# Attention over a sorted graph: VectorE weights edge one-hots two blocks at a time, ScalarE converts all node one-hots, stored as 8-bit floats beside the sum layers

## The chip, the cores and the metric

The kernel runs on one core of one Trainium2 chip. The metric is the device time of the whole program in microseconds, as the median of repeated executions. Beside the times there is one profiled execution, whose trace gives the start and the duration of every instruction. The engines are called PE (TensorE; PEld is its weight load), DVE (VectorE), ACT (ScalarE), POOL (GpSimd) and SP (the queue that issues most DMAs).

## The reference, cut to what matters

A graph of 6250 nodes with 128 features and 100,000 edges, sorted by destination, goes through four blocks, each a layer norm, a ReLU and a graph network, added to x: a mean over neighbours, a product over edges, three sum layers (mean over neighbours, two matrices each), and three attention layers. The last two are what matters here.

```python
def _sage_layer(x, src, dst, Wl, Wr, bias, n_nodes):          # the sum layers
    msg_sum = segment_sum(x[src], dst); cnt = segment_sum(1, dst)
    return (msg_sum / maximum(cnt, 1)) @ Wl + x @ Wr + bias

def _gat_conv(x, src, dst, ea, W, a_src, a_dst, We, a_edge, bias):   # attention, with self loops
    h = x @ W
    alpha = leaky_relu((h @ a_src)[s] + (h @ a_dst)[d] + ea_full @ We @ a_edge, 0.2)
    ex = exp(alpha - segment_max(alpha, d)[d])
    coef = ex / (segment_sum(ex, d)[d] + 1e-16)
    return segment_sum(h[s] * coef[:, None], d) + bias
```

The graph is the same in all three attention layers; only the coefficients change.

## The kernel before, in words

**The attention layers** (`attention_split`, `split_edges`). The edges are split. The destinations of the "late" edges are handled by gathering rows of a table from DRAM (POOL, L67), running a recurrence over them on DVE (`late`, `acc`, `ex`, `top`) and storing the history. The destinations of the "early" edges are handled with matrix products, and this is the part that the change touches. Their nodes lie in 5 groups (GP) of 128 windows; a window has 5 nodes (NW) and up to 128 edges (WCAP). For each window two one-hot matrices pick things out: `hot` has, for each edge, a one in the column that its source belongs to (125 columns of nodes), and the node one-hot has, for each edge, a one in column k*50+l of 250, where k is the destination within the window and l the rest of the source's number. `cnt = (hot * coef)^T @ node one-hot` is then a small weighted adjacency, which ACT merges into `m` (`merged`, L2607), and `product` (L2447) multiplies `m` with the features `hst` held in SBUF.

A loop of 160 steps per layer (480 in all) treats four windows a step. The windows alternate between two number formats: k = 0 is done in full F32, k = 1 in F32R as a high and a low part (`coef_h`, `coef_l`, so there is a third weighted one-hot, `hot_l`). `ready(step + 2)` makes the operands two steps ahead, into tiles with three buffers. Before the change, for each of the four windows it makes

- the node one-hot `hot_n`: for k = 0 DVE compares `l_slot` with the edge's place (`lt.id_t`, F32; L116), 250 elements; for k = 1 ACT converts an 8-bit one-hot `half_n` loaded from DRAM (L2435);
- the weighted edge one-hot `hot_c`: ACT multiplies the 8-bit `hot` with the coefficient of each edge (L2436), 125 elements;

and once a step, for both k = 1 windows together, DVE makes `hot_l` (L112, 250 elements). `nodes_ready` issues the loads: `hot` every second step, `half_n` every step (L2416, 62.5 KB).

Within a step the program order is: PE's products into `cnt` (two PSUM buffers), the start of a product unit, ACT's merge of the step before, `ready(step + 2)`, some matmuls of the product, the source terms or the softmax of the next group, then the gathers and the late recurrence. On PE, DVE and ACT this order is fixed: a function `chain` ties each instruction to the one before it on its engine. ACT thus takes the exponential of the late recurrence (L2502) in turn with the merges and the one-hots. The gathers on POOL are tied to PE's progress (`clocked`).

**Beside the sum layers** (`woven`). The one-hots don't depend on the features, so they are made earlier, by `early_edges`, while the three sum layers run. `woven` cuts each unit of a sum layer (four node tiles: some 120 matmuls into `o`, L1544) into 15 pieces and puts a piece of the side work, one `next(beside)`, after 9 of them; the end of the unit before (`node_terms`: `agg` on DVE, `nt` on PE, L1564, and then its norm or its split into parts) is spread over the first pieces. Again the order on PE, DVE and ACT is as written. The sum layers read their adjacency from DRAM through `piece` loads on SP (L1643), six buffers ahead, and ACT converts a part of them (`as_f`, L1653). Another recurrence on DVE (`s_acc`) uses gathered rows.

For each of the 80 blocks of 8 windows, `early_edges` makes on DVE `ee_hot` (8 compares of 128), `ee_col` (one TENSOR_TENSOR of 400 elements with both operands spread over two axes), `ee_node` (4 compares of 250, the k = 1 windows alone; L2028) and `ee_hot_t`, and stores each with a DMA on SP. All of these are tiles with two buffers. `slot_b` is the bf16 row 0, 1, 2, ... ; `place` holds each edge's column k*50+l and is transposed, per group, into `lt.id_t`.

Of the kernel before, what the change touches and what calls it, by code (L numbers as in the profile page):

```python
# [9 lines left out]
F32 = mybir.dt.float32  # L10
BF16 = mybir.dt.bfloat16
# [40 lines left out]
def kernel(ctx: ExitStack, tc: tile.TileContext, a: dict, out: bass.AP):  # L52
# [58 lines left out]
    def tt(o, x, y, op):  # L111
        nc.vector.tensor_tensor(o, x, y, op)  # L112
# [1715 lines left out]
    hot_t_dram = [dram.tile([128, 128 * 128], F8, name=f"hot_t{g}") for g in range(GP)]  # L1828
    col_dram = [dram.tile([128, 128 * T], F8, name=f"col{g}") for g in range(GP)]
    of_dram = [dram.tile([128, NW * WCAP], BF16, name=f"of{g}") for g in range(GP)]  # L1830
    node_dram = [dram.tile([128, 64 * T * NW], F8, name=f"node{g}") for g in range(GP)]
    ale_dram = [[dram.tile([128, WCAP], F32, name=f"ale{i}_{g}") for g in range(GP)] for i in range(3)]
    ade_dram = [dram.tile([PL * C2, 1], F32, name=f"ade{i}") for i in range(3)]
    part_dram = [dram.tile([128, WCAP], U8, name=f"part{g}") for g in range(GP)]
# [7 lines left out]
    class Late:  # L1842
# [3 lines left out]
        def __init__(self, pool):  # L1846
            self.y_t = pool.tile([128, T, P], F32, name="y_t")
            self.src = pool.tile([128, C2], I32, name="l_src")
            self.same = pool.tile([PL, C2], F32, name="l_same")
            self.pen = pool.tile([PL, C2], F32, name="l_pen")  # L1850
            self.first = pool.tile([PL, 1], I32, name="l_first")
            self.fix = pool.tile([PL, 1], I32, name="l_fix")
            self.flow_t = pool.tile([PL, PL], F32, name="l_flow_t")
            self.pen_t = pool.tile([PL, PL], F32, name="l_pen_t")
            self.end = pool.tile([128, T2], I32, name="l_end")
            self.q = pool.tile([R2, T2], F32, name="l_q")
            self.c = pool.tile([R2, T2], F32, name="l_c")
            self.slot = pool.tile([128, C2], F32, name="l_slot")
            self.id_t = pool.tile([128, GP, 128], F32, name="l_id_t")
            self.vecs = [pool.tile([128, 6], F32, name=f"l_vecs{i}") for i in range(3)]  # L1860
            self.w_ext = [pool.tile([128, W], F32, name=f"l_w_ext{i}") for i in range(3)]
            self.v = [pool.tile([128, 3], F32, name=f"l_v{i}") for i in range(3)]
            self.e_self = [pool.tile([128, 1], F32, name=f"l_e_self{i}") for i in range(3)]
            self.als = pool.tile([128, 3, 2, T], BF16, name="l_als")
# [162 lines left out]
    def one_hot(o, x, at):  # L2027
        nc.vector.tensor_scalar(o, x, at, None, op0=OP.is_equal, saturate=False)  # L2028

    def early_edges(lt):  # L2030

        with tc.tile_pool(name="ee", bufs=1) as pool, tc.tile_pool(name="ee_ps", bufs=1, space=PSUM) as ps:
# [59 lines left out]
            for g in range(GP):  # L2092
# [41 lines left out]
                yield  # L2134
                hi_t = f32("hi_t", 128)
                lo_t = pool.tile([128, 128], BF16, name="ee_lo_t")
                for x, x_t in ((hi, hi_t), (lo, lo_t), (place, lt.id_t[:, g, :])):
                    t_ps = ps.tile([128, 128], F32, name="ee_t")
                    transpose(t_ps, x)
                    nc.vector.tensor_copy(x_t, t_ps)  # L2140
                    yield
                rows = rows_of(g, 0)
                for w0 in range(0, 128, WB):
                    hot = pool.tile([128, WB, 128], F8, name="ee_hot", bufs=2)
                    for w in range(WB):
                        one_hot(hot[:, w, :], slot_b[:, :128], hi_t[:, w0 + w:w0 + w + 1])
                    nc.sync.dma_start(hot_dram[g][:, w0 * 128:(w0 + WB) * 128], hot.rearrange("p w h -> p (w h)"))
                    col = pool.tile([128, WB, T], F8, name="ee_col", bufs=2)
                    nc.vector.tensor_tensor(col, slot_b[:, None, :T].to_broadcast([128, WB, T]),
                                            lo_t[:, w0:w0 + WB, None].to_broadcast([128, WB, T]), OP.is_equal, saturate=False)  # L2150
                    nc.sync.dma_start(col_dram[g][:, w0 * T:(w0 + WB) * T], col.rearrange("p w l -> p (w l)"))
                    yield
                    node = pool.tile([128, WB // 2, T * NW], F8, name="ee_node", bufs=2)
                    for w in range(0, WB, 2):
                        n = w0 + w + 1
                        one_hot(node[:, w // 2, :], slot_b, lt.id_t[:, g, n:n + 1])
                    nc.sync.dma_start(node_dram[g][:, w0 // 2 * T * NW:(w0 + WB) // 2 * T * NW],
                                      node.rearrange("p w n -> p (w n)"))
                    hot_t = pool.tile([128, WB * WCAP], F8, name="ee_hot_t", bufs=2)
                    one_hot(hot_t, rows, here[:, 0:1])  # L2160
                    nc.sync.dma_start(hot_t_dram[g][:, w0 * 128:(w0 + WB) * 128], hot_t)
                    if w0 + WB < 128:
                        rows = rows_of(g, w0 + WB)
                    yield
# [105 lines left out]
    def split_edges(lt, i, first, wp, pool, ps, mv, sc):  # L2270
# [138 lines left out]
        def nodes_ready(step):  # L2409

            g, w0 = step // 32, step % 32 * 4
            if w0 % WB == 0:
                lt.hot = pool.tile([128, WB, 128], F8, name="hot")
                nc.sync.dma_start(lt.hot.rearrange("p w h -> p (w h)"), hot_dram[g][:, w0 * 128:(w0 + WB) * 128])
            half_n = pool.tile([128, 2, T * NW], F8, name="half_n")
            nc.sync.dma_start(half_n.rearrange("p w n -> p (w n)"),  # L2416
                              node_dram[g][:, w0 // 2 * T * NW:(w0 + 4) // 2 * T * NW])
            return half_n

        def ready(step, half_n=None):  # L2420

            g, w0 = step // 32, step % 32 * 4
            if half_n is None:
                half_n = nodes_ready(step)
            hot_n = [pool.tile([128, 2, T * NW], of, name=f"hot_n{k}", bufs=3) for k, of in enumerate((F32, F32R))]
            hot_c = [pool.tile([128, 2, P], of, name=f"hot_c{k}", bufs=3) for k, of in enumerate((F32, F32R))]
            hot_l = pool.tile([128, 2, P], F32R, name="hot_l", bufs=3)
            hot = lt.hot[:, w0 % WB:w0 % WB + 4, :P]
            coef, high, low = coef_t[g]
            for w in range(4):  # L2430
                k, h = w % 2, w // 2
                if k == 0:
                    ts(hot_n[k][:, h, :], lt.slot[:, :T * NW], lt.id_t[:, g, w0 + w:w0 + w + 1], OP.is_equal)
                else:
                    nc.scalar.activation(hot_n[k][:, h, :], half_n[:, h, :], AF.Copy)  # L2435
                nc.scalar.activation(hot_c[k][:, h, :], hot[:, w, :], AF.Copy,  # L2436
                                     scale=(high if k else coef)[:, w0 + w:w0 + w + 1])
            tt(hot_l, hot.rearrange("p (h k) c -> p k h c", k=2)[:, 1],
               low[:, w0:w0 + 4].rearrange("p (h k) -> p k h", k=2)[:, 1, :, None].to_broadcast([128, 2, P]), OP.mult)
            return hot_n, hot_c, hot_l  # L2440
# [704 lines left out]
```

## Time and profile before

| what | value |
|---|---|
| median of 13 runs | 4818.59 us (4804.71 to 4827.85) |
| the profiled execution | 4828.39 us |
| its span, first to last instruction | 4825.9 us, mean granted clock 0.895 |
| busy: PE, PEld, DVE | 4163.7, 2991.3, 4042.7 us |
| busy: ACT, POOL | 3308.4, 2849.0 us |
| sum layers (about 1880 to 2800 us), busy PE, DVE, ACT | 882, 679, 437 of 920 us |
| attention layers and the end (2800 to 4826 us), busy PE, DVE, ACT | 1801, 1700, 1514 of 2026 us |
| attention loops, first to last merge | 2862.8 to 3435.3, 3523.2 to 4095.3, 4184.4 to 4754.5 us |

How to read the lines of the profile: a row of the table of stretches gives the stretch, its length, each engine's busy time with the number of its instructions, the granted PE clock, the mean busy share of the 16 DMA engines and GB/s. A group gives line, engine and operation, out<-in by the program's names, the shapes and the count; then busy time and mean ns of one; then the idle time of the engine just before these instructions and what ended it. A wait line gives who waited for whom: us in total, times, longest. A line of the order of time gives start, us and the instruction. L112, L116, L118 and L121 are helpers (`tt`, `ts` and `stt`) that many places call, so there one goes by tile names. DVE and ACT instructions overlap at their ends, so that the mean of one is longer than the distance from start to start.

### The profile page before, as it was taken

The numbers are of one execution on the slowest core, as the hardware profiler recorded it, in microseconds if no ns is written. First come the engines' busy times: TensorE is split into PE (matmuls) and PEld (weight loads), VectorE is DVE, ScalarE is ACT, GpSimd is POOL, SyncE is SP. The second block draws the span as 40 slices with busy tenths as digits, with TensorE's granted clock in tenths as the row PEclk, the third lists the DMA queues.
The fourth block names the chain that finished last, engine by engine and source line by source line (L and its number), as shares of the span: only waits on it lengthen the run. The fifth ranks groups of instructions, "written<-read, shape, count | busy, mean of one in ns | idle before, by whom it ended". The sixth has DMA issues, their size and how long they took to land. (4 is left out here: it accounts for less than half of the span.)

```text
span 4825.9 us, 84662 instructions
## 1 busy us (share of the span) xinstructions
PE 4163.7 (86%) x25786; PEld 2991.3 (62%) x25786; DVE 4042.7 (84%) x12029; ACT 3308.4 (69%) x6467; POOL 2849.0 (59%) x2848
## 2 busy tenths in 40 slices
PE   1499998888888869999999979999789999799996
PEld 0255543434444435555555569889778898698895
DVE  7999869999999964678868869899698897798985
ACT  5466658888888856543345568778577787687784
POOL 1365007777777754656737537677377776477772
PEclk9999996666666659999999989999999999899998
DMA  4344236666666647899989955555455554465553
GB/s 99 102 153 163 92 118 215 206 203 201 197 202 206 184 131 226 265 282 279 297 243 297 282 167 160 157 154 155 138 150 156 156 159 132 148 164 154 156 148 106
DMA packets 577362, 868.53 MB, mean 180 GB/s; under 512 B 206555, under 2 KB 451739, under 8 KB 568450
## 3 DMA queue, kind: packets, MB, share of 16 engines
q1 hardware_dynamic: 483459, 674.15, 44.5%
q0 software_dynamic: 91104, 186.95, 15.8%
q8 instruction: 205, 3.36, 0.3%
q10 hardware_dynamic: 2332, 1.93, 0.2%
q14 instruction: 262, 2.15, 0.1%
HBM read 563.92 MB, written 298.68 MB: 179 GB/s over the span
## 5 line engine op out<-in xcount | busy, mean ns | idle before, releaser
L67 POOL DMA_INDIRECT rows<-gtable,l_src x1176 | 1187.2, 1010 | 547.5 <-issue 277.0
L67 POOL DMA_INDIRECT rows<-table,f_src x784 | 781.5, 997 | 282.2 <-issue 181.6
L2447 PE MATMUL o<-m,hst 125*128 125x160 f32 x6000 | 917.1, 304 | 0.0
L2624 PE MATMUL cnt<-hot_n,hot_c 128*125 128x250 f32 x2880 | 758.7, 361 | 121.0 <-ACT m L2607 117.2
L67 POOL DMA_INDIRECT s_rows<-table,s_src x660 | 661.3, 1002 | 340.7 <-issue 168.5
L2447 PEld LDWEIGHTS o<-m,hst 125*128 125x128 f32 x6000 | 856.0, 194 | 0.0
L1653 ACT ACTIVATE as_f<-piece 128x1000 fp32r<-128x1000 fp8e4 x390 | 381.5, 1029 | 278.0 <-DMA piece<-adj 180.8
L2624 PEld LDWEIGHTS cnt<-hot_n,hot_c 128*125 128x125 f32 x2880 | 452.1, 193 | 158.4 <-ACT m L2607 128.7
L2607 ACT ACTIVATE m<-cnt 125x1000 f32<-125x1000 f32 x480 | 474.3, 988 | 17.0 <-PE cnt L2624 15.8
L923 PE MATMUL z<-w,s 128*128 128x128 f32 x1568 | 348.1, 391 | 152.5 <-DVE s L121 148.1
L2623 PE MATMUL cnt<-hot_n,hot_l 128*125 128x250 f32 x960 | 454.6, 474 | 0.0
L121 DVE SCALAR_TENSOR_TENSOR acc<-acc,ex,rows 128x130 f32<-128x130 f32 x1173 | 414.4, 353 | 33.8
L923 PEld LDWEIGHTS z<-w,s 128*128 128x128 f32 x1568 | 295.3, 281 | 232.3 <-DVE s L121 231.9
L1544 PE MATMUL o<-as_f,of_two 128*128 128x500 f32 x1560 | 415.6, 412 | 12.7 <-ACT as_f L1653 12.5
L1407 ACT ACTIVATE adj<-cnt 128x1000 fp8e4<-128x1000 f32 x250 | 305.4, 1222 | 174.4 <-PE cnt L1406 168.5
L2435 ACT ACTIVATE hot_n<-half_n 128x250 fp32r<-128x250 fp8e4 x960 | 386.4, 402 | 28.2 <-DMA half_n<-node 27.5
L2436 ACT ACTIVATE hot_c<-hot,coef_t 128x125 f32<-128x125 fp8e4 x960 | 375.6, 391 | 0.1
L2436 ACT ACTIVATE hot_c<-hot,coef_h 128x125 fp32r<-128x125 fp8e4 x960 | 374.9, 391 | 0.0
L902 PE MATMUL z<-bf,w 128*128 128x512 f32 x392 | 354.2, 1002 | 9.0 <-ACT bf L868 9.0
L1544 PE MATMUL o<-adj,parts 128*128 128x500 fp8e4 x1500 | 357.0, 376 | 0.1
L1544 PEld LDWEIGHTS o<-as_f,of_two 128*128 128x128 f32 x1560 | 296.4, 192 | 84.0 <-ACT as_f L1653 16.4
L868 ACT ACTIVATE soft<-z 128x512 f32<-128x512 f32 x392 | 222.2, 586 | 164.5 <-PE z L923 164.0
(628 smaller groups left out, 8114.9 us busy)
## 6 DMA issues: line engine op xcount, KB each, us to landing
piece<-adj SPq DMA_DIRECT2D x360, 250.0 KB
late_hist<-acc SPq DMA_DIRECT2D x147, 455.0 KB
dist<-ew_dram SPq DMA_DIRECT2D x48, 1024.0 KB
sum_hist<-s_acc SPq DMA_DIRECT2D x132, 320.0 KB
adj<-adj SPq DMA_DIRECT2D x10, 3125.0 KB
hot<-hot SPq DMA_DIRECT2D x240, 128.0 KB
half_n<-node SPq DMA_DIRECT2D x480, 62.5 KB
ea<-in_edge_attr SPq DMA_DIRECT2D x54, 512.0 KB
```

Of the source, the lines that this page charges most:

```text
L67: return nc.gpsimd.indirect_dma_start(out=dst, out_offset=None, in_=table, in_offset=bass.IndirectOffsetOnAxis(ap=idx, axis=0))
L121: nc.vector.scalar_tensor_tensor(o, x, s, y, op0=op0, op1=op1)
L902: nc.tensor.matmul(z1, lhsT=w1, rhs=st["bf"][:, i % 2 * HB:(i % 2 + 1) * HB, :], start=False, stop=True)
L923: nc.tensor.matmul(z2[:, j, :], lhsT=s1[:, j, :], rhs=w2, start=False, stop=j == HB - 1)
L1544: yield nc.tensor.matmul(o[:, :n], lhsT=parts.columns(l, 1, s)[:, 0, :], rhs=adj(l), start=(l == 0 and s == 0), stop=(l == T - 1 and s == ...
L1653: nc.scalar.activation(made[-1], piece[:, at:at + n], AF.Copy)
L2435: nc.scalar.activation(hot_n[k][:, h, :], half_n[:, h, :], AF.Copy)
L2436: nc.scalar.activation(hot_c[k][:, h, :], hot[:, w, :], AF.Copy, scale=(high if k else coef)[:, w0 + w:w0 + w + 1])
L2447: nc.tensor.matmul(o, lhsT=hst[:, l, :D], rhs=m[:P, l, :], start=(l == 0), stop=(l == T - 1))
L2607: nc.scalar.activation(m[:P, :, :, u * 4:u * 4 + 4].rearrange("p l k q -> p k l q"), cnt[:P, :, :T * NW].rearrange("p w (k l) -> p k l w", ...
L2623: nc.tensor.matmul(o, lhsT=hot_l[:, h, :], rhs=hot_n[k][:, h, :], start=True, stop=False)
L2624: nc.tensor.matmul(o, lhsT=hot_c[k][:, h, :], rhs=hot_n[k][:, h, :], start=k == 0, stop=True)
```

## The change

It has two halves that belong together.

1. `early_edges` makes and stores the node one-hots of all 8 windows of a block instead of the four with k = 1. It no longer uses four compares with one number per partition, but two TENSOR_TENSOR compares of four windows each (128 x 1000 elements, 8-bit result), which compare `slot_b` with the edges' places held in bf16 (`id_b`). Each of the two results is stored with its own DMA. `ee_node` keeps two buffers of 1000 bytes a partition; the DRAM tensors `node` double, and `lt.id_t` goes.
2. `ready` no longer compares on DVE nor weights on ACT. ACT converts the node one-hots of both formats (two instructions of 500 elements, from `half_n` with four windows, 125 KB a load); DVE weights the edge one-hots (two TENSOR_TENSOR products of 2 x 125 elements, as `hot_l` has been made).

```diff
@@ early_edges
-                for x, x_t in ((hi, hi_t), (lo, lo_t), (place, lt.id_t[:, g, :])):
+                id_b = pool.tile([128, 128], BF16, name="ee_id_b")
+                for x, x_t in ((hi, hi_t), (lo, lo_t), (place, id_b)):
...
-                    node = pool.tile([128, WB // 2, T * NW], F8, name="ee_node", bufs=2)
-                    for w in range(0, WB, 2):
-                        n = w0 + w + 1
-                        one_hot(node[:, w // 2, :], slot_b, lt.id_t[:, g, n:n + 1])
-                    nc.sync.dma_start(node_dram[g][:, w0 // 2 * T * NW:(w0 + WB) // 2 * T * NW],
-                                      node.rearrange("p w n -> p (w n)"))
+                    for n0 in range(w0, w0 + WB, 4):
+                        node = pool.tile([128, 4, T * NW], F8, name="ee_node", bufs=2)
+                        nc.vector.tensor_tensor(node, slot_b[:, None, :].to_broadcast([128, 4, T * NW]),
+                                                id_b[:, n0:n0 + 4, None].to_broadcast([128, 4, T * NW]), OP.is_equal, saturate=False)
+                        nc.sync.dma_start(node_dram[g][:, n0 * T * NW:(n0 + 4) * T * NW], node.rearrange("p w n -> p (w n)"))
@@ nodes_ready
-            half_n = pool.tile([128, 2, T * NW], F8, name="half_n")
-            nc.sync.dma_start(half_n.rearrange("p w n -> p (w n)"),
-                              node_dram[g][:, w0 // 2 * T * NW:(w0 + 4) // 2 * T * NW])
+            half_n = pool.tile([128, 4, T * NW], F8, name="half_n")
+            nc.sync.dma_start(half_n.rearrange("p w n -> p (w n)"), node_dram[g][:, w0 * T * NW:(w0 + 4) * T * NW])
@@ ready
-            for w in range(4):
-                k, h = w % 2, w // 2
-                if k == 0:
-                    ts(hot_n[k][:, h, :], lt.slot[:, :T * NW], lt.id_t[:, g, w0 + w:w0 + w + 1], OP.is_equal)
-                else:
-                    nc.scalar.activation(hot_n[k][:, h, :], half_n[:, h, :], AF.Copy)
-                nc.scalar.activation(hot_c[k][:, h, :], hot[:, w, :], AF.Copy,
-                                     scale=(high if k else coef)[:, w0 + w:w0 + w + 1])
+            by = hot.rearrange("p (h k) c -> p k h c", k=2)
+            for k, of in enumerate((coef, high)):
+                nc.scalar.activation(hot_n[k], half_n.rearrange("p (h k) n -> p k h n", k=2)[:, k], AF.Copy)
+                tt(hot_c[k], by[:, k], of[:, w0:w0 + 4].rearrange("p (h k) -> p k h", k=2)[:, k, :, None].to_broadcast([128, 2, P]), OP.mult)
             tt(hot_l, hot.rearrange("p (h k) c -> p k h c", k=2)[:, 1], ...
```

More of the change, by code (lines that the diff above doesn't have):

```diff
@@ L1830 @@
     of_dram = [dram.tile([128, NW * WCAP], BF16, name=f"of{g}") for g in range(GP)]
-    node_dram = [dram.tile([128, 64 * T * NW], F8, name=f"node{g}") for g in range(GP)]
+    node_dram = [dram.tile([128, 128 * T * NW], F8, name=f"node{g}") for g in range(GP)]
     ale_dram = [[dram.tile([128, WCAP], F32, name=f"ale{i}_{g}") for g in range(GP)] for i in range(3)]
@@ L1858, in __init__ @@
             self.slot = pool.tile([128, C2], F32, name="l_slot")
-            self.id_t = pool.tile([128, GP, 128], F32, name="l_id_t")
             self.vecs = [pool.tile([128, 6], F32, name=f"l_vecs{i}") for i in range(3)]
```

## The prediction

> **What bounds the kernel now.** I read the busy shares first: PE 86%, DVE 84%, ACT 69% of the span. No engine bounds the whole, so I cut the trace into stretches and took those in which the changed lines run: the sum layers (1880 to 2800 us, the `ee_` lines from 2054 on) and the three attention layers (2800 to 4800 us, each with a loop of 160 steps). The table of stretches, busy us of PE, PEld, DVE, ACT, POOL:
>
> ```profile
> core 0: us, PE busy (x) PEld busy (x) DVE busy (x) ACT busy (x) POOL busy (x), PEclk, DMA share, GB/s
> 2890.00:3290.00 400.00, 376.83 (x3588) 360.08 (x3587) 362.98 (x1088) 312.75 (x861) 287.48 (x284) 0.98 0.59 159
> 3290.00:3435.00 145.00, 134.76 (x889) 129.06 (x888) 111.33 (x365) 117.41 (x322) 89.81 (x90) 0.96 0.50 133
> ...
> 2195.00:2430.00 235.00, 235.00 (x1080) 131.53 (x1079) 190.36 (x627) 84.55 (x97) 157.30 (x160) 1.00 0.94 295
> ```
>
> The first row is most of an attention loop (108.5 steps of 3.69 us): PE and DVE are both over 90%, ACT is at 78%. The last is the middle sum layer: PE never rests. Next, who waits in the attention stretch (us in total, times, longest):
>
> ```profile
> ACT ex L2502 <- DVE ex L121: 54.0, 26, 4.2
> ...
> PE cnt L2624 <- ACT m L2607: 20.4, 11, 5.1
> ...
> DVE z_w L121 <- ACT z_w L2450: 5.7, 5, 3.1
> ```
>
> PE's one large wait names ACT, but ACT itself stands 54 us behind DVE's `ex`. The chain is DVE, then ACT's exponential, then ACT's merge `m`, then PE. So DVE, not ACT, is the engine that is late. In the sum layers the order of time shows the same engine on the path: one DVE run without a rest, and the PE matmul that needs its end.
>
> ```profile
> 2079.52 1.23 DVE L2028 TENSOR_SCALAR ee_node<-ee_slot_b,l_id_t 128x250 fp8e4<-128x250 bf16 x4
> ...
> 2085.21 1.20 DVE L2028 TENSOR_SCALAR ee_node<-ee_slot_b,l_id_t 128x250 fp8e4<-128x250 bf16 x4
> ...
> 2091.07 1.35 DVE L2028 TENSOR_SCALAR ee_node<-ee_slot_b,l_id_t 128x250 fp8e4<-128x250 bf16 x4
> ...
> 2095.07 0.67 DVE L112 TENSOR_TENSOR agg<-o,inv 128x500 f32<-128x500 f32 x1
> ...
> 2095.79 1.10 PE L1564 MATMUL nt<-agg,w_a 128*128 128x500 f32 x2
> ```
>
> agg ends at 2095.74 and PE's nt starts 0.05 us later: PE was waiting, though its row is called busy.
>
> **Part 1, stored node one-hots (L2155, beside the sum layers).** Per block of 8 the change removes four compares of 250 elements and adds two TENSOR_TENSORs of 1000. The rows, mean ns of one:
>
> ```profile
> L2028 DVE TENSOR_SCALAR ee_node<-ee_slot_b,l_id_t 128x250 fp8e4<-128x250 bf16 x320 | 96.1, 362 | 0.5 <-DMA node<-ee_node 0.5
> L2149 DVE TENSOR_TENSOR ee_col<-ee_slot_b,ee_lo_t 128x400 fp8e4<-128x400 bf16 x80 | 44.8, 560 | 0.0
> ```
>
> I count from start to start, since DVE instructions overlap at their ends: the four take 1.04 to 1.19 us together, 1.12. ee_col has the new instruction's form (bf16 operands spread over two axes, 8-bit result); its 400 elements take 0.48 us, one element in 1.04 ns (0.42 us) plus 0.06. So 1000 take 1.10 us, two 2.20: **+1.1 us a block, 80 blocks, +88 us of DVE**. Most blocks lie in runs like the one above. For each of the 22 `agg` from 2030 to 2763 I went back to DVE's last wait over 0.6 us and counted the ee_node groups in between, and took off the time from agg's end to nt. Seven agg end 0.05 us before nt and have 2, 3, 4, 2, 4, 4 and 3 groups behind them: 24.2 us, less 1.2 of short waits inside, 23. Eight have 0.2 to 3.4 us to spare and 3 or 4 groups: 16 left. The others stand right behind a wait, which takes the addition up. **+39 us** on the path; bounds 15 (some runs recover) and 88 (all).
>
> The stores double: 160 DMAs of 125 KB instead of 80, 10.2 MB more, in stretches whose DMA share is 0.92 to 0.94. ee_node keeps two buffers but uses two a block, so an instruction waits for the store one block back instead of two. Packets of 1000 B, put to their issues in order, show the last landing 5.3 us after DVE's end in the median (1.7 to 10.0); blocks are 5.8 us apart in dense runs, 6.9 with the addition. So some will wait. The nearest row is ee_node's own 0.5 us of waiting (bound below 0); with today's landings and the longer period the shortfalls add up to about 35 (bound above). I take **+10**. On SP each second store is one more instruction (0.32 us) ahead of the next `piece` load, which ACT already awaits; PE's wait for it through `as_f` is only 12.5 us, and it stays hidden unless DMA saturates. The copies of `place` into id_b replace those into id_t one for one.
>
> A stall of PE may cost more than its length. The nt at 2064.53 took 2.03 us after a wait of 3.84 (the others 1.00 to 1.11), with a granted clock of 0.86 in that stretch; the nt at 2444.75 took 1.11 after 3.79. [...]
>
> **Part 2, the attention step (480 of them).** DVE gives up two compares of 250 and takes two products of 250 in exactly the form of hot_l. ACT gives up 2 conversions and 4 weightings and takes 2 conversions of 500.
>
> ```profile
> 3010.18 0.60 DVE L116 TENSOR_SCALAR hot_n<-l_slot,l_id_t 128x250 f32<-128x250 f32 x2
> ...
> 3010.69 0.41 DVE L112 TENSOR_TENSOR hot_l<-hot,coef_l 128x250 fp32r<-128x250 fp8e4 x1
> ...
> 3011.02 0.57 DVE L112 TENSOR_TENSOR one<-x_ps,col 128x400 f32<-128x400 f32 x1
> ...
> L2435 ACT ACTIVATE hot_n<-half_n 128x250 fp32r<-128x250 fp8e4 x960 | 386.4, 402 | 28.2 <-DMA half_n<-node 27.5
> L2436 ACT ACTIVATE hot_c<-hot,coef_t 128x125 f32<-128x125 fp8e4 x960 | 375.6, 391 | 0.1
> ```
>
> Start to start, two hot_n take 0.51, one hot_l 0.33. DVE: 0.66 - 0.51 = **+0.15 us a step**. ACT's six start 0.29 to 0.30 apart, 1.77 together; 250 elements take 0.30 and the 1000 of `m` 0.89, so 500 take 0.50 and two 1.00: **-0.77 us a step**, 370 us of ACT in all. By the reading above ACT's gain is not on the path. In the 400 us stretch DVE is idle for 37: 19 are waits with a name, 18 are gaps of some 30 ns that go with its instructions. It gets 108.5 x 0.15 = 16.3 more. If all named waits go, 363 + 18 + 16 = 397, nothing is lost; if all stay, 416. ACT's part of them (z_w 5.7, coef_l 5.6) should mostly go, the rest stay: 405 to 408, say +6. The first 27 us of the loop have DVE at 25.75 busy: 7.5 steps x 0.15 = 1.1. In the tail (second row) DVE has 34 us of idle and takes 6 in; PE's waits there hang on the gathered rows, not on ACT. So +7 a layer, **+20** for three; bounds -37 (397 in each stretch and the tail's 9.3 us of waiting for `m` gone) and +55 (416 and the starts). The new wait on DVE is hot_c's for `hot` and the coefficients; hot_l, behind the same loads, has it now for 1.8 us in all, and behind it stand acc and the terms of the next group, which nobody needs within a step. The step's load goes from 62.5 to 125 KB, 30 MB more at a DMA share of 0.59, issued two steps ahead: hidden, and ACT now has room to wait.
>
> **Sum:** 39 + 10 + 20 = +69 us. The profiled execution took 4828.39 us (span 4825.9, 2.5 around it), so 4897 of its kind; it is 9.8 above the median of 4818.59, so **4888 us** as a median.
>
> **Rivals.**
> 1. ACT's relief decides, faster. All PE waits for `m` go: 20.4 + 9.3 us a layer, 89. For it: ACT is named in every one of them. Against: ACT waits for DVE at the same places. It decides if DVE's 0.15 us a step fits into its idle 0.34. With the 39 of part 1: -50, about 4769.
> 2. The sum layers hide part 1, as their DVE was only 74% busy (679 of 920 us) and PE could run ahead: attention's +20 alone, 4839. The seven agg with no time to spare speak against it. If ACT's relief also pays for the 20, it is no change.
> 3. The stores hold DVE: with one block's distance it waits the whole 35, 39 + 35 = 74 in the sum layers, and attention takes its upper 55: 4948. For it: DMA shares of 0.94 to 1.01 in the 25 us stretches with dense blocks. Against: ee_hot, with two blocks' distance, waits 0.2 us in all for its store.
>
> **Chances.** Forecast 0.58, rival 1 0.18, rival 2 0.10, rival 3 0.14. About 0.2% (9.6 us) is what a measurement can tell from no change. Rival 1 lies wholly on the faster side: 0.18. Same takes 0.07, out of rival 2. Slower: 0.75. The bounds of the terms give 15 + 0 - 37 = -22 (4797) and 88 + 10 + 35 = +133 (4952); I take 4795 to 4955, which leaves out most of rival 1 and some of rival 3.
>
> **What will show it.** Right: ee_node 128x1000 at about 1.19 us each; nt waits for agg (21.6 us over the sum layers now) growing by some 40, that stage about 50 longer; in the loops ACT near 57%, DVE at 93% or more, the 400 us stretches 405 to 410, and PE still waiting for `m` behind `ex`. Wrong: loops shorter than 572 us with fewer waits for `m` (rival 1), nt starting on time (rival 2), ee_node waiting for node by tens of us (rival 3), or a 1000-element instruction much off 1.1 us.

## The result and the profile after

The changed kernel takes **4908.62 us** (median of 8 runs, 4901.51 to 4925.33) against 4821.99 us of the kernel before (37 runs, 4804.71 to 4833.46): the ratio is **1.0188, 95% interval 1.0176 to 1.0201**, so it is slower by 87 us. Its profiled execution took 4913.53 us, with a span of 4911.6; the span of before was 4825.9, so 85.7 us more are to be found.

I found the place by the first and the last merge `m` of each attention loop, as the trace has them:

| us | before | after | difference |
|---|---|---|---|
| start to first merge (all before attention) | 2862.8 | 2925.7 | +62.9 |
| loops, first to last merge | 572.5, 572.1, 570.0 | 579.1, 579.2, 582.9 | +26.5 |
| between the loops, and the end | 248.6 | 244.8 | -3.8 |

**The sum layers.** I bounded the part in which the new instructions run by the same two matmuls of the program in both traces, the nt of the unit at 2064.53 and the last nt but one (2766.40 before). The table of stretches gives, of before:

```profile
2064.53:2766.40 701.87, 680.26 (x3050) 405.41 (x3051) 551.35 (x1863) 324.04 (x375) 408.33 (x410) 0.98 0.92 282
```

and of the changed kernel, between the same two matmuls:

```profile
2063.10:2829.81 766.71, 702.87 (x3051) 414.24 (x3052) 632.81 (x1707) 323.69 (x375) 470.88 (x411) 0.95 0.90 271
```

The stretch is 64.8 us longer, and the row splits it in two. PE is idle for 766.7 - 702.9 = 63.8 us (21.6 before), that is 42.2 more. And PE is **busy for 22.6 us more with the same matmuls**, at a granted clock of 0.95 where it was 0.98. The waits of the whole sum layers say who PE waited for. The largest of PE's before:

```profile
PE nt L1564 <- DVE agg L112: 21.6, 6, 11.4
```

and in the changed kernel (PE's two largest, then one of DVE's):

```profile
PE nt L1564 <- DVE agg L112: 65.7, 16, 11.4
PE o L1544 <- ACT as_f L1653: 11.8, 5, 3.7
...
DVE ee_node L2155 <- DMA node<-ee_node: 16.6, 20, 2.3
```

nt waits 44 us longer for agg than before (in the stretch between the two matmuls 53.6 us against 9.6). The last line is new: DVE stands before its own stores. That PE is also slow for a while behind a wait is seen in the order of time, PE alone, in the changed kernel:

```profile
2405.44 1.00 PE L1563 MATMUL nt<-own,w_r 128*128 128x500 f32 x2
2413.34 2.04 PE L1564 MATMUL nt<-agg,w_a 128*128 128x500 f32 x2 [6.90 <-DVE agg L112]
2415.17 3.13 PE L1544 MATMUL o<-piece,y_t 128*128 128x500 fp8e4 x7
2417.74 2.69 PE L1544 MATMUL o<-as_f,of_two 128*128 128x500 f32 x8
2420.27 0.81 PE L1544 MATMUL o<-piece,y_t 128*128 128x500 fp8e4 x3
```

and at a like place of the kernel before:

```profile
2409.16 1.00 PE L1563 MATMUL nt<-own,w_r 128*128 128x500 f32 x2
2410.00 1.00 PE L1564 MATMUL nt<-agg,w_a 128*128 128x500 f32 x2
2410.84 1.64 PE L1544 MATMUL o<-piece,y_t 128*128 128x500 fp8e4 x7
2412.14 2.16 PE L1544 MATMUL o<-as_f,of_two 128*128 128x500 f32 x8
2414.14 0.81 PE L1544 MATMUL o<-piece,y_t 128*128 128x500 fp8e4 x3
```

From the start of nt to the three matmuls of 0.81 it is 4.14 us before and 6.93 after: behind the wait of 6.90, another 2.8 us go because the matmuls run slowly for a while (nt 2.04 us in place of 1.00, the first seven into `o` 3.13 in place of 1.64).

**The attention loops.** The counterpart of the 400 us row of before (this one has some 108 steps), and its waits (ACT, PE, DVE):

```profile
2950.00:3350.00 400.00, 369.76 (x3543) 351.31 (x3542) 369.25 (x1077) 233.16 (x421) 293.03 (x283) 0.98 0.64 174
```

```profile
ACT ex L2496 <- DVE ex L121: 88.5, 29, 7.1
...
PE cnt L2618 <- ACT m L2601: 22.7, 11, 5.5
...
DVE z_w L121 <- ACT z_w L2444: 4.1, 4, 2.2
```

ACT has become light (58% where it was 78%), DVE is busier (369 of 400 where it was 363), and ACT's waiting for DVE's `ex` has grown from 54.0 to 88.5 us. In this stretch ACT has 79.6 us less to do, and it spends them waiting: 34.5 us more for `ex`, 19.9 more for PE's products (`m` for `cnt`: 4.9 before, 24.8 now), 10.1 more for its loads `half_n` (3.2 and 13.3), the rest in smaller waits. PE waits for `m` about as long as before. The groups of the new instructions, over the whole program:

```profile
L2155 DVE TENSOR_TENSOR ee_node<-ee_slot_b,ee_id_b 128x1000 fp8e4<-128x1000 bf16 x160 | 185.0, 1192 | 16.8 <-DMA node<-ee_node 16.6
...
L2430 ACT ACTIVATE hot_n<-half_n 128x500 f32<-128x500 fp8e4 x480 | 294.8, 614 | 45.3 <-DMA half_n<-node 44.9
```

### The profile page after: what moved, and what is told of

It is laid out like the page before. It is cut to its first block, busy times and chain, and to the rows that moved or that the text cites. A ratio compares the mean times of both kernels' runs of the same rounds, so it can differ in the third digit from the quotient of the medians.

```text
span 4911.6 us, 82418 instructions
## 1 busy us (share of the span) xinstructions
PE 4192.3 (85%) x25786; PEld 3001.2 (61%) x25786; DVE 4171.2 (85%) x11869; ACT 2970.6 (60%) x4547; POOL 2948.6 (60%) x2848
## 5 line engine op out<-in xcount | busy, mean ns | idle before, releaser
L67 POOL DMA_INDIRECT rows<-gtable,l_src x1176 | 1220.4, 1038 | 542.6 <-issue 281.2
L67 POOL DMA_INDIRECT s_rows<-table,s_src x660 | 722.4, 1095 | 338.7 <-issue 165.4
L2430 ACT ACTIVATE hot_n<-half_n 128x500 f32<-128x500 fp8e4 x960 | 538.5, 612 | 45.3 <-DMA half_n<-node 44.9
L1544 PE MATMUL o<-as_f,of_two 128*128 128x500 f32 x1560 | 421.7, 417 | 13.0 <-ACT as_f L1653 11.8
L118 DVE TENSOR_SCALAR run<-acc,f_same,f_fresh 128x128 f32<-128x128 f32 (+1 forms) x783 | 312.4, 399 | 14.4
L1544 PE MATMUL o<-piece,of_three 128*128 128x500 fp8e4 x1200 | 293.2, 388 | 1.7 <-ACT of_three L1121 1.2
```

The lines of the kernel that those rows point to most:

```text
L67: return nc.gpsimd.indirect_dma_start(out=dst, out_offset=None, in_=table, in_offset=bass.IndirectOffsetOnAxis(ap=idx, axis=0))
L118: nc.vector.tensor_scalar(o, x, s1, s2, op0=op0, op1=op1)
L1544: yield nc.tensor.matmul(o[:, :n], lhsT=parts.columns(l, 1, s)[:, 0, :], rhs=adj(l), start=(l == 0 and s == 0), stop=(l == T - 1 and s == ...
L2430: nc.scalar.activation(hot_n[k], half_n.rearrange("p (h k) n -> p k h n", k=2)[:, k], AF.Copy)
```

## The experiments

Twelve kernels were run. For the first eight, the table has the time as a ratio to the kernel before on the same chip, the stretch between the same two matmuls of the sum layers, and the sum of the three loops. The stretch comes from one profile each: in e2, whose sum layers are those of before, it is 9 us shorter than in before, so differences under 10 us in that column say nothing.

| run | ratio (95%) | sum-layer stretch | loops |
|---|---|---|---|
| before | 1 | 701.9 | 1714.6 |
| after | 1.0188 (1.0176 to 1.0201) | 766.7 | 1741.2 |
| e1_store_all | 1.0158 (1.0127 to 1.0189) | 772.4 | 1720.7 |
| e2_weigh_alone | 1.0055 (1.0033 to 1.0076) | 692.8 | 1745.4 |
| e3_four_buffers | 1.0177 (1.0151 to 1.0204) | 750.9 | 1743.3 |
| e4_act_weighs_k0 | 1.0075 (1.0054 to 1.0096) | 765.0 | 1683.4 |
| e5_stores_twice | 1.0088 (1.0057 to 1.0120) | 747.6 | 1713.7 |
| e6_compare_more | 1.0093 (1.0062 to 1.0123) | 748.8 | 1709.5 |
| e7_hot_at_once | 1.0187 (1.0152 to 1.0222) | 762.9 | 1747.9 |
| e8_piece_earlier | 1.0187 (1.0157 to 1.0217) | 758.4 | 1748.5 |

The last four, e9 to e12, have numbers of their own below: in their session the kernel before itself took 5352.33 us, and the profiles of these four have waits on PE, DVE and ACT that they put to no instruction of the program. So they are compared with the kernel before, and with each other, within that session only.

The theory that the runs were to test is that of the prediction: VectorE is the engine that is late, in the sum layers ahead of agg and in attention ahead of `ex`. The rivals: ScalarE is the limit of the loop; the stores and their DMA traffic, not VectorE's time, are the cost beside the sum layers.

### Each half alone: e1_store_all and e2_weigh_alone

e1 keeps the stored one-hots of all windows and their larger loads, and takes `ready` back to what it was. The lines that it adds to the changed kernel:

```diff
+                    if x is place:
+                        nc.vector.tensor_copy(lt.id_t[:, g, :], t_ps)
@@ ready
+                if k == 0:
+                    ts(hot_n[k][:, h, :], lt.slot[:, :T * NW], lt.id_t[:, g, w0 + w:w0 + w + 1], OP.is_equal)
+                else:
+                    nc.scalar.activation(hot_n[k][:, h, :], half_n[:, w, :], AF.Copy)
+                nc.scalar.activation(hot_c[k][:, h, :], hot[:, w, :], AF.Copy,
+                                     scale=(high if k else coef)[:, w0 + w:w0 + w + 1])
```

> All eight node one-hots are made and stored as in the changed kernel, and loaded with 125 KB a step, but the attention step works as before (DVE compares for k = 0, ACT converts every second stored one-hot and weights). In the changed kernel's trace the first attention step starts 63 us later and the three loops together are 26 us longer. Theory (the two halves add up, each by DVE): the first step as late as with the whole change, loops of 572 us as before, so before + 60 to 66, ratio 1.013. Rival (the doubled loads of half_n, not DVE, lengthen the loops): loops near 579 and about + 85, ratio 1.018.

e2 is the reverse: `early_edges` and the loads of before, the step of the change. It leaves out the node one-hots of k = 0 and converts those of k = 1 twice; the work of a step is the same. Against the step of the change:

```diff
@@ ready
-                nc.scalar.activation(hot_n[k], half_n.rearrange("p (h k) n -> p k h n", k=2)[:, k], AF.Copy)
+                nc.scalar.activation(hot_n[k], half_n, AF.Copy)
```

> The attention step as in the changed kernel, but the sum layers as before: only every second node one-hot is made and stored (62.5 KB loads), and each is used for both formats, so the even windows have wrong node one-hots; the work is the same. Theory (DVE's +0.15 us a step is on the path, ACT's -0.77 is not): first step at 2855 as before, loops + 20 to 27 us in all, ratio 1.004 to 1.006. Rival (ACT's relief counts, what lengthened the loops are the loads): loops shorter than before, ratio under 1.000.

e1 costs 1.58% (76 us) and e2 0.55% (26 us); their sum is somewhat above the 1.88% of the change, within their intervals. In e1 the loops come back to 6 us above before (1720.7) and the sum layers stay long; in e2 it is the other way round. The halves are separate, and the one in the sum layers is the larger. That e2 is slower, although it takes 0.77 us a step from ScalarE, refutes the rival that ScalarE is the limit of the loop.

### Who is late in the loop: e4_act_weighs_k0

The changed kernel, but ScalarE weights the edge one-hots of k = 0 again:

```diff
+                if k:
                     tt(hot_c[k], by[:, k], of[:, w0:w0 + 4].rearrange("p (h k) -> p k h", k=2)[:, k, :, None].to_broadcast([128, 2, P]), OP.mult)
+                else:
+                    for h in range(2):
+                        nc.scalar.activation(hot_c[k][:, h, :], hot[:, 2 * h, :], AF.Copy, scale=of[:, w0 + 2 * h:w0 + 2 * h + 1])
```

> The changed kernel, but ACT weights the two k = 0 edge one-hots (two instructions of 125 elements a step): DVE gives up one product (-0.33 us a step, which is 0.18 less than before the change), ACT takes 0.59 more (0.18 less than before). Theory (DVE is the late engine of the loop): the loops fall below those of before, 565 us or less against 579 in the changed kernel, so 40 us or more off the changed kernel, ratio to before 1.010 or less. Rival (ACT's share decides): loops between 579 and 572 or longer than in the changed kernel, ratio 1.014 to 1.02.

One TENSOR_TENSOR of 250 elements (0.33 us start to start) less a step on VectorE, and the loops are 58 us shorter than in the changed kernel, 31 shorter than before. A 400 us stretch of its first loop, and its waits:

```profile
2960.00:3360.00 400.00, 383.15 (x3648) 366.88 (x3647) 352.49 (x1018) 306.98 (x671) 303.19 (x296) 0.99 0.66 181
```

```profile
ACT ex L2500 <- DVE ex L121: 45.7, 27, 4.7
...
PE cnt L2622 <- ACT m L2605: 16.6, 10, 3.6
```

PE gets 383 us of work done where it got 370, DVE needs 352 where it needed 369, ACT is at 77% and still waits 46 us for DVE. This is the theory's clearest support: time given to ScalarE costs nothing here, time taken from VectorE comes back (58 of 480 x 0.33 = 158 us).

### What holds the sum layers: e3, e5, e6

e3 gives `ee_node` four buffers instead of two.

```diff
-                        node = pool.tile([128, 4, T * NW], F8, name="ee_node", bufs=2)
+                        node = pool.tile([128, 4, T * NW], F8, name="ee_node", bufs=4)
```

> The changed kernel with four buffers of ee_node instead of two, so that a compare waits for the store of two blocks back, as before the change. Theory (DVE's 16.6 us of waiting for these stores is partly on the path): the waits go, and the time falls by 6 to 14 us against the changed kernel, ratio to before 1.016 to 1.017. Rival (DMA is the bound and the stores only move): no change, ratio 1.019.

The waits for the store (16.6 us) are gone and the stretch is 16 us shorter, but the time is the changed kernel's within its interval. The two buffers cost between nothing and some 16 us.

e5 takes the kernel before and stores each `ee_node` tile twice, into a doubled DRAM tensor: the DMA work of the change without its VectorE work. e6 takes the kernel before and adds a compare of 1000 elements a block that is stored nowhere (with the places in bf16, `id_b`, as in the change): the VectorE work (80 x 1.1 us) without its DMAs.

```diff
@@ e5
-                    nc.sync.dma_start(node_dram[g][:, w0 // 2 * T * NW:(w0 + WB) // 2 * T * NW],
-                                      node.rearrange("p w n -> p (w n)"))
+                    for w in (w0, w0 + 128):
+                        nc.sync.dma_start(node_dram[g][:, w // 2 * T * NW:(w + WB) // 2 * T * NW],
+                                          node.rearrange("p w n -> p (w n)"))
@@ e6
+                    more = pool.tile([128, 4, T * NW], F8, name="ee_more", bufs=1)
+                    nc.vector.tensor_tensor(more, slot_b[:, None, :].to_broadcast([128, 4, T * NW]),
+                                            id_b[:, w0:w0 + 4, None].to_broadcast([128, 4, T * NW]), OP.is_equal, saturate=False)
```

> The kernel before, in which each ee_node tile is stored twice, to two halves of a doubled DRAM tensor: 80 DMAs of 125 KB more on SP's queue beside the sum layers, as many bytes as the change adds there, and not one instruction more on VectorE. The attention layers are those of before. Theory (the added time beside the sum layers is VectorE's, on its way to agg): 0 to +8 us against before, about 4823, first merge within 8 us of 2863, nt's waits for agg near 22 us. Rival (the stores: DMA traffic, SP's queue ahead of the piece loads, late releases): +20 us or more, first merge after 2882.

> The kernel before with one more TENSOR_TENSOR compare of 1000 elements a block on VectorE (80 in all, about 1.1 us each, as many microseconds as the change adds there), into a scratch tile that is stored nowhere. No DMA more, attention as before. Theory (VectorE's time alone): +39 to +63 us, about 4858 to 4882, first merge 2902 to 2926, nt's waits for agg up by some 40 us. Rival (stores): less than +10 us. If it lands between, both have a part.

Both cost: e5 0.88% (42 us), e6 0.93% (45 us). The theory had nothing for e5 and the rival nothing for e6, so **neither is whole**. The stretch and PE's waits in it, of e5:

```profile
2062.87:2810.51 747.64, 693.86 (x3051) 405.13 (x3051) 550.56 (x1863) 323.61 (x375) 405.48 (x410) 0.98 0.90 278
```

```profile
PE o L1544 <- ACT as_f L1653: 25.7, 18, 3.8
PE nt L1564 <- DVE agg L112: 18.9, 11, 4.3
PE o L1544 <- DMA piece<-adj: 8.5, 10, 2.3
```

and of e6:

```profile
2070.96:2819.75 748.79, 695.23 (x3050) 411.78 (x3051) 634.68 (x1945) 322.84 (x375) 428.76 (x410) 0.96 0.87 264
```

```profile
PE nt L1564 <- DVE agg L112: 37.9, 14, 5.3
PE o L1544 <- ACT as_f L1653: 17.8, 7, 4.4
```

They have the same length but not the same waits. (In the same stretch of before, PE waits 9.6 us for agg, 12.5 for `as_f` and 0.3 for `piece`.) In e6, PE waits for agg: VectorE. In e5 the waits lead to the loads: for `piece`, and for `as_f`, which itself waits longer for `piece` (281 us in this stretch; 170 before). A part goes by way of VectorE, whose work is that of before: it now waits 26.4 us for the loads of `ee_rows` (3.3 before), and PE's waits for agg grow by 9 us.

The last two columns suggest why: before, the DMAs moved 282 GB/s at a share of 0.92, that is 198 MB in 701.9 us; e5 moves 208 MB at 278 GB/s. Ten MB more at a rate that doesn't rise are, as an estimate, 10.2 / 0.282 = 36 us, of the 46 measured. That the bytes are the cause is argued, not shown. The mean of 282 GB/s is not the most that these DMAs move: between 2550 and 2575 us of before they moved 328, at a share of 1.01. And each added store is also one more instruction on SP ahead of the loads: SP's DMA instructions take 427 us of the stretch in e5 and 381 in before. No run adds the bytes without the instructions. In the stretch of before, then, VectorE and the loads were both just about in time, and each has its own way to PE.

Together they cost less than the sum in the profiles: 46 + 47 = 93 us for the two alone, 63 to 71 in after, e1 and e4. While PE waits for one, the other catches up: ACT's `as_f` waits 107 us for `piece` in the changed kernel, where it is 170 before and 281 in e5. The times (0.88 + 0.93 against 1.58%, up to 1.89) don't exclude the plain sum.

### Two cures that cured nothing: e7_hot_at_once and e8_piece_earlier

e7 makes `ee_hot` with one TENSOR_TENSOR instead of eight compares; e8 moves one side piece of each unit to where VectorE has time.

```diff
@@ e7
-                    for w in range(WB):
-                        one_hot(hot[:, w, :], slot_b[:, :128], hi_t[:, w0 + w:w0 + w + 1])
+                    nc.vector.tensor_tensor(hot, slot_b[:, None, :128].to_broadcast([128, WB, 128]),
+                                            hi_t[:, w0:w0 + WB, None].to_broadcast([128, WB, 128]), OP.is_equal, saturate=False)
@@ e8
-                if at in (0, 2, 4, 6, 8, 10, 11, 12, 13):
+                if at in (0, 1, 2, 4, 6, 8, 10, 12, 13):
```

> The changed kernel, with ee_hot made by one TENSOR_TENSOR of 8 x 128 elements (from a bf16 copy of hi) in place of eight compares of 128. Eight compares take about 1.6 us a block start to start, one of 1024 elements about 1.1 us: VectorE gets some 0.5 us a block less, 40 us over 80 blocks. Theory (VectorE on the way to agg): 15 to 25 us faster than the changed kernel, about 4885 to 4894, and nt's waits for agg 15 to 25 us smaller. Rival (stores): within 5 us of the changed kernel.

> The changed kernel, with one side piece of each sum-layer unit moved: after pieces 0, 1, 2, 4, 6, 8, 10, 12, 13 of the unit in place of 0, 2, 4, 6, 8, 10, 11, 12, 13. Same instructions, same DMAs, only the order differs: one piece of VectorE's side work stands behind agg early in the unit, where VectorE has been seen to wait, and not in the dense end ahead of the next agg. Theory (agg is late because side work stands ahead of it in VectorE's order): 15 to 30 us faster than the changed kernel, about 4879 to 4894, nt's waits for agg under 50 us. If only totals mattered (VectorE's busy time, the bytes stored): no difference, within 8 us.

Both took the time of the changed kernel (4911.18 and 4909.05 us; their intervals leave room for a gain of some 15 to 17 us, the low end of what the theory gave). Here my theory, as it stood, fell. e7 did take 34 us from VectorE in the stretch (632.8 to 599.0), but nt's waits for agg fell only from 53.6 to 44.6. DVE's own waits in this stretch of e7 show where the rest went:

```profile
DVE ee_node L2155 <- DMA node<-ee_node: 24.9, 24, 3.0
DVE s_acc L121 <- DMA s_rows<-table,s_src: 18.5, 19, 1.8
```

In the changed kernel they were 16.2 and 7.0: VectorE came earlier to the next thing that a DMA had to bring. In e8 the wait that I aimed at fell by more than half, as forecast, but another took its place:

```profile
PE o L1544 <- ACT as_f L1653: 37.2, 9, 8.5
PE nt L1564 <- DVE agg L112: 23.2, 7, 6.9
```

(11.8 and 53.6 in the changed kernel.) This fits two limits close to each other: if the stores alone hold the stretch near the 748 us of e5, taking work from VectorE can win back no more than the rest of the 767.

### The gathers, and putting it together: e9 to e12

In the changed kernel the gathers that POOL issues beside the sum layers take 1156 ns in the mean, 995 before. The order of time shows one of the long ones:

```profile
2428.75 2.30 DVE L2155 TENSOR_TENSOR ee_node<-ee_slot_b,ee_id_b 128x1000 fp8e4<-128x1000 bf16 x2
...
2429.96 1.90 POOL L67 DMA_INDIRECT s_rows<-table,s_src  x1 [0.31 <-issue]
```

It ends 0.81 us after the end of the TENSOR_TENSOR (2431.05). In e6 all 11 of these gathers that began inside the added compare and took over 1.3 us ended 0.81 or 0.82 us after it; the 65 that began inside ee_node's TENSOR_SCALAR compares in the kernel before took 1.00 us in the mean. e9 therefore makes the same one-hots with TENSOR_SCALARs (and `id_b` in F32).

```diff
-                        nc.vector.tensor_tensor(node, slot_b[:, None, :].to_broadcast([128, 4, T * NW]),
-                                                id_b[:, n0:n0 + 4, None].to_broadcast([128, 4, T * NW]), OP.is_equal, saturate=False)
+                        for w in range(4):
+                            one_hot(node[:, w, :], slot_b, id_b[:, n0 + w:n0 + w + 1])
```

> The changed kernel, with ee_node made by eight TENSOR_SCALAR compares of 250 elements a block (one number per partition, as before the change) in place of two TENSOR_TENSORs of 1000; same stores, same VectorE time (8 x 0.28 = 2.24 us against 2.20), attention as changed. What it tells apart: in the changed kernel a gather that POOL issues while a TENSOR_TENSOR runs ends 0.82 us after that instruction's end, and the gathers of the sum layers take 1.16 us in the mean (1.00 before). If these held gathers cost time: gathers back near 1.0 us, and 8 to 20 us faster than the changed kernel (about 4889 to 4901). If VectorE's time and the stores are all of it: gathers back near 1.0 us, but within 6 us of the changed kernel.

The gathers are back at 985 ns. The ratio is 1.0066 (1.0044 to 1.0087), but in a session in which all kernels took 11% longer, and the changed kernel was not run in it. Within the session the sum-layer stretch of e9, between the same two matmuls as in the table, is 47 us longer than that of e10, which has the sum layers of before (799.8 against 753.1). Whether the held gathers cost time is **left open**.

What holds a gather is not the kind of compare. The changed kernel's own trace has a TENSOR_SCALAR of 1024 elements that does it too:

```profile
2069.37 0.75 DVE L2027 TENSOR_SCALAR ee_hot_t<-ee_rows,ee_here 128x1024 fp8e4<-128x1024 uint8 x1
2069.46 1.47 POOL L67 DMA_INDIRECT s_rows<-table,s_src  x1 [0.30 <-issue]
```

Again the gather ends 0.81 us after the end of the compare (2070.12). So it was for 38 of the 40 gathers there that began inside an `ee_hot_t`; the other two began 14 and 19 ns after its start and took 0.95 and 0.96 us. What e9 changes is the length: its compares are short (0.28 us from start to start), so a gather that is held until the end of one loses little.

e10 and e11 are the kernel before, with one and with both blocks of `hot_l` weighted on ScalarE:

```diff
-            tt(hot_l, hot.rearrange("p (h k) c -> p k h c", k=2)[:, 1],
-               low[:, w0:w0 + 4].rearrange("p (h k) -> p k h", k=2)[:, 1, :, None].to_broadcast([128, 2, P]), OP.mult)
@@ e10
+            nc.scalar.activation(hot_l[:, 0, :], hot[:, 1, :], AF.Copy, scale=low[:, w0 + 1:w0 + 2])
+            ts(hot_l[:, 1, :], hot[:, 3, :], low[:, w0 + 3:w0 + 4], OP.mult)
@@ e11
+            for h in range(2):
+                nc.scalar.activation(hot_l[:, h, :], hot[:, 2 * h + 1, :], AF.Copy, scale=low[:, w0 + 2 * h + 1:w0 + 2 * h + 2])
```

> The kernel before (sum layers untouched), in which the low part hot_l is no longer one TENSOR_TENSOR of 250 elements on VectorE: ScalarE weights one of its two blocks (0.29 us more a step), VectorE the other with a TENSOR_SCALAR of 125 (about 0.15 us less a step). Theory (VectorE is the late engine of the attention loop, ScalarE has room): loops 4 to 8 us shorter each, 10 to 25 us faster than before, about 4796 to 4810. Rival (ScalarE is as near its limit as its 78% and the waits for its merges suggest): loops 5 us longer each or more, 15 us slower than before or more.

> The kernel before, in which ScalarE weights both blocks of hot_l: VectorE 0.33 us less a step, ScalarE 0.58 us more (from about 2.9 to 3.5 us of a 3.6 us step). Theory: ScalarE takes over as the late engine; the loops end within 10 us of those of before, so 4800 to 4850, with the waits for the merge m growing and those for VectorE's ex gone. If ScalarE had ample room, it would be 25 us or more faster; if ScalarE already was the limit, 50 us or more slower.

Ratios 1.0010 (0.9989 to 1.0030) and 1.0029 (1.0003 to 1.0054): neither the gain of the theory nor the loss of the rival. But the loop was another one in that session. Its 400 us row in e10:

```profile
3200.00:3600.00 400.00, 345.28 (x3060) 319.28 (x3058) 298.84 (x932) 294.27 (x824) 245.86 (x244) 0.95 0.52 136
```

No engine is over 87% busy, and PE stands some 380 us of the whole span in waits that the profile puts to nothing (59 in the profile of before). DVE, at 75%, is far from full here, so the two runs don't test the theory, and what happened in that session I can't say.

e12 joins what had helped: the changed kernel with e4's weighting, four buffers and e9's compares.

> The changed kernel with three edits that the earlier runs point to: ScalarE weights the edge one-hots of k = 0 (the loops were 58 us shorter by it), ee_node has four buffers (the first merge came 12 us earlier), and its compares are TENSOR_SCALARs of 250 elements. By the sum of these: 4854.8 less 12, less 0 to 20, so 4822 to 4843: the stored one-hots still cost some 40 us beside the sum layers against 31 us won in the loops, no faster than before. A result under 4810 would say that the sum layers had room all along.

Ratio **0.9988 (0.9970 to 1.0006)**: no difference from the kernel before. In its session the loops sum to 1991 us against 2026 and 2032 of e10 and e11, some 35 to 41 shorter, and the sum-layer stretch is 36 us longer (789.0 against 753.1 in e10). In that session, what the stored one-hots win in attention, with the work split well, is what they cost beside the sum layers. No version that beats the kernel before was found.

## Why the prediction was right, and where it was not

It gave 4888 us in a range of 4795 to 4955; 4908.62 was measured, and slower was the likely side. Its sum was +69 us for a profiled execution; the spans differ by 85.7. Step by step:

1. **VectorE, not ScalarE, is the late engine of the loop.** Right: e2 is slower than before, e4 faster than the changed kernel. ScalarE's 370 us went into waiting, and the largest part of it, in the stretch shown, into waiting for `ex` (54.0 to 88.5 us).
2. **+20 for attention** (6 in the stretch, 1.1 at the start, 0 in the tail, for each layer). Measured 26.5. From the tenth to the 117th merge the loops grew by 4.6, 5.3 and 6.6 us, the starts by 0.8 to 1.0; the tails, put at nothing, by 1.2, 0.8 and 5.5. The last of these is most of the difference, and it comes back in e2, e3, e7 and e8, which weight in the same way (5.3 to 8.5 us). In the changed kernel DVE waits there 13.8 us for gathered rows (10.0 before); that is a part of it, and the rest is not explained.
3. **The instruction itself.** Put at 1.10 us from start to start and 1.19 long; measured 1.11 and 1192 ns, from the group of `ee_col`, which had the same form. From 400 elements in 0.48 us to 1000 in 1.11 it is 1.05 ns an element, where the sum took 1.04.
4. **+39 on the path ahead of agg.** nt's waits for agg grew by 44 us, but it is partly luck that the count of blocks behind each agg came so near. (Between 2030 and 2763 us stand 24 agg, not 22; the seven and the eight of the sum are as counted.) In e6, which adds VectorE's work alone, these waits grow by 28 us (9.6 to 37.9 in the stretch) and the stretch by 47. In e3, where DVE no longer waits for its stores, they are 38.3 too; so the rest of the 44 came by way of those waits. As a theory of the stage it was too simple: e7 and e8 show that taking VectorE's work away again doesn't give it back.
5. **"+10" for the stores, and the transfers "hidden unless DMA saturates".** This step failed. I asked only whether ee_node would wait for its own buffer (it did, for 16.6 us). e5 shows that the stores cost some 42 us by themselves, for the most part by way of the `piece` loads. That the DMAs were busy nearly all the time stood in the row that I had shown: a share of 0.94 at 295 GB/s. The sum came out near all the same because, in the profiles, the two costs largely lie beside each other: where VectorE already holds PE, the loads catch up. The prediction did not give this reason for its +10, so that it came near here is luck.
6. **PE's slow matmuls, for which the sum had no term.** PE's busy time grew by 22.6 us, at a granted clock of 0.95 (0.98 before). I took the nt at 2444.75 of before for one behind which PE was not slow; so it was for two matmuls, and the next seven took 0.57 to 0.62 us where 0.37 to 0.39 is usual. In the stretch there are 15 such trains of slow matmuls in the changed kernel and 5 in before, so, as an estimate, some 2.3 us each. This is rough: by the same division e6 (13 trains, 15.0 us more PE busy) gives 1.9 and e5 (8 trains, 13.6 us more) 4.5.

In the stretch of the changed kernel all eight waits of 3.05 us or more were followed by slow matmuls, and five of the eight between 2.2 and 2.9. A wait of 1.90 us (at 2683.18 of before) was followed by them too, and so was a pair of 1.35 and 1.22 us (at 2159.23 and 2160.78 of the changed kernel). So a count of the longest stalls alone misses some.

The rivals: the first (ScalarE decides) is refuted by e2. The second (hidden in the sum layers) by nt's waits. The third (the stores hold DVE) had the right subject and the wrong mechanism: DVE waits 16.6 us for its stores, not 35; in e5 the larger part of the stores' cost is on the way from the loads to PE.

## What to carry to other kernels

Ask of a stage not only which engine is late, but how far behind it the next limit is: here adding to VectorE alone or to the stores alone cost some 42 to 45 us each, and taking from VectorE alone gave nothing back that could be measured. A DMA share of 0.92, as in the stretch of before, is a warning even where hardly a wait of PE names a load yet: ask of added stores what they do to the loads that are issued behind them, not only whether their own buffers come free in time. When work can be shared between two engines, find the late one from who waits for whom: one TENSOR_TENSOR a step on VectorE or on ScalarE decided between 27 us lost and 31 us won in the loops. And price each PE stall with the slow matmuls behind it, here, by the estimate above, some 2 us for each train of them on top of the wait.

## What the runs showed of the hardware

- **Some VectorE instructions hold up POOL's gathers.** In the changed kernel, a gather that begins inside one that holds it ends no sooner than 0.81 us after its end; the 420 that began while VectorE was idle took 0.94 us. Of the gathers that began at least 0.2 us before the end of the VectorE instruction, all 66 inside `ee_node`'s TENSOR_TENSOR (two operands in SBUF) were held: 58 ended 0.81 to 0.82 us after its end, the other eight later, four of them 0.82 us after the end of the next `ee_node`. Inside `ee_hot_t`'s TENSOR_SCALAR 38 of 40 were held, all but the two that began within 0.02 us of its start. Of the 61 inside `one<-x_ps,col`, a TENSOR_TENSOR with one operand in PSUM, none was (0.94 us). What decides which instructions hold a gather, no run here shows.
- **The slow matmuls** after a stall come in trains of 2 to 12 matmuls into `o` (changed kernel), most of them at 0.62 us where 0.37 to 0.39 is usual, and can begin 0.9 to 1.4 us after the wait is over (at 2444.75 and 2683.18 of before).
- The DMAs' mean rate in the sum-layer stretch was 282 GB/s before and 278 in e5, which asks for 10 MB more in it: the stretch became longer, not the rate higher.
